# Splitting the tiled products of a linear-attention kernel into two runs

## The chip, the core and the metric

The kernel runs on one core of a Trainium2 chip. The metric is the time of one execution on the device in microseconds: 306.25 us, median of three runs (306.08 to 306.49). The core's engines that matter here are TensorE (PE, with its weight loads shown as PEld), VectorE (DVE), ScalarE (ACT), GpSimd (POOL) and SyncE (SP), which here only issues transfers. Each engine works through a queue of its own, and semaphores order the engines among each other.

## What is computed

The reference is a transformer stack of 12 layers of attention without softmax, followed by a layer norm, a gated FFN and another layer norm, on 16 sequences of 256 tokens with 128 features and 16 heads of 8 features. Cut to what matters:

```python
for i in range(12):
    q, k, v = split(x @ Wqkv[i].T + bqkv[i])          # 16 heads of 8
    att = einsum('bhqd,bhkd->bhqk', q, k) / sqrt(8)    # no softmax
    y = einsum('bhqk,bhkd->bhqd', att, v)
    x = y @ Wproj[i].T + bproj[i] + x
x = layernorm(x0 + x)
x = layernorm(x + (silu(x @ wg.T) * (x @ wu.T)) @ wd.T)
```

## The kernel before

Without a softmax a layer is linear in the tokens once `k` and `v` are summed over them. So the kernel never holds a layer's tokens. For every sequence it keeps a 128x128 matrix that maps the centred input tokens to the layer's tokens, and one more column for the offset (`tst`, 130 columns wide with padding; `thl` is its split into a high and a low part), and the Gram matrix of the input tokens (`g`). Two sequences form a pair (`PB = 2`), there are eight pairs (`NP`), and four pairs form a half (`G = 4`, `NO = 2` halves of eight sequences).

In each layer, and for each half, TensorE does the following work. "Full-size" are products that use all 128 rows and 128 columns of the array:

- **kv** (lines 436 to 438): six full-size products for each pair, which map `k` and `v` weights through the pair's matrices.
- **gv** (line 457): the Gram matrix times v's map, two fp32 products for each pair.
- **q** (lines 444 to 446): three full-size products for each pair, for q's map.
- **M** (line 501): k's map times the Gram product, that is keys against values, but only the diagonal blocks of 32x32 features. For a half these are 4 pairs x 2 sequences x 4 blocks = 32 matmuls, each on 128 rows and 32 columns of the array, so that four can lie side by side. They all write one bank, `pm`.
- **Offsets' products** (line 382, "riders"): eight small matmuls (twelve in layer 0), on 128x32 tiles too, that give the offsets of q, k and v for a half of this or of a later layer. They are issued in front of an M run.
- **y** (line 519): M, masked to heads (`gm`), times q's map. 2 sequences x 4 pairs x 4 blocks = 32 matmuls on 32x32 tiles of the array, sixteen of which can lie side by side. They write four banks, `pys`, one for each pair.
- **w** (lines 536 to 538): the output projection, three full-size products for each pair.

Between them VectorE, ScalarE and GpSimd move results out of the banks: `kv`, `gv` and `q` by copies (lines 205 and 207), M by an addition and a multiplication with the mask (lines 511 and 213) into `gm`, y by a split into `yhl` (lines 205 or 207, then 532), the projection by an addition to `tst` (line 543) with a split into `thl` (lines 205 and 210).

The order of all this isn't written by hand. Each step is an `Op` of a `Plan`, with its cost on each engine that may do it (in ns), what it reads and writes, and a priority. `Plan.run` goes through the steps like a simulator: it takes the step that can start first, by its own clock, breaks ties by priority, emits its instructions there and then, and so fixes the order on each engine, the engine where there's a choice, and the bank (eight of them). For a step on TensorE that follows another TensorE step it depends on, it takes a pause of 30 ns; after the other engines 300 ns. An M run with its riders is one step (cost 890 plus 140 for each rider), and so is a y run (cost 1200). A step's instructions are never mixed with those of another step on TensorE.

The riders of a half `o` in layer `l` are `(l, o)` for the first two layers, and `(l + o, 1 - o)` where that sum is from 2 to 11. So M has one rider in most runs, two in the second half of layer 1, and none in the second half of layer 11. What follows an M run's riders is in `offsets` (lines 385 to 405), ending with the addition on line 402 or 404.

When the eleven layers after layer 0 are done, `ffn` handles the eight pairs (line 575 on), which begins during layer 11.

Of the kernel before, what the change touches and what calls it, by code (L numbers as in the profile page):

```python
# [21 lines left out]
C = 128  # L22
# [3 lines left out]
PB = 2  # L26
NP = B // PB
W = C + 2
# [8 lines left out]
G = 4  # L37
# [13 lines left out]
LSTEP = 0.05  # L51
WLEAD = 0.6
TAILW = 0.0001
AHEAD = 0.16
SPARE = 500

# [17 lines left out]
PE, ACT, DVE, POOL, SP = "pe", "act", "dve", "pool", "sp"  # L74
AFTER = {PE: 270, ACT: 160, DVE: 200, POOL: 180, SP: 3000}
TO_PE = 300


class Val:


    def __init__(self, kind=None):
        self.kind, self.slot = kind, None
        self.writers, self.readers, self.ops, self.left = [], [], [], 0


class Op:
    def __init__(self, n, costs, emit, prio):
        self.n, self.costs, self.emit, self.prio = n, costs, emit, prio
        self.end = self.engine = None  # L90
        self.deps, self.users, self.vals = set(), [], []


class Plan:
    def __init__(self, slots):
        self.slots, self.ops = slots, []

    def op(self, costs, emit, reads=(), writes=(), prio=0.0):

        o = Op(len(self.ops), costs, emit, prio)  # L100
        for v in reads:
            o.deps.update(v.writers)
        for v in writes:
            o.deps.update(v.writers, v.readers)
            v.writers, v.readers = [o], []
        for v in reads:
            if v not in writes:
                v.readers.append(o)
        o.vals = list(dict.fromkeys([*reads, *writes]))
        for v in o.vals:  # L110
            if v.kind:
                v.left += 1
                v.ops.append(o)
        for d in o.deps:
            d.users.append(o)
        self.ops.append(o)

    def run(self):
        free = dict.fromkeys(AFTER, 0.0)
        free.update({SP: 800.0, DVE: 4000.0, ACT: 3200.0, POOL: 4900.0})  # L120
        slots = {k: [(0.0, i) for i in range(n)] for k, n in self.slots.items()}
        left = {o: len(o.deps) for o in self.ops}
        for o in reversed(self.ops):
            o.tail = min(o.costs.values()) + 300 + max((u.tail for u in o.users), default=0)
        ready = [o for o in self.ops if not left[o]]
        takes = lambda o: [v for v in o.vals if v.kind and v.slot is None]
        while ready:
            found = []
            for o in ready:
                if any(not slots[v.kind] for v in takes(o)):  # L130
                    continue
                held = max((min(slots[v.kind])[0] for v in takes(o)), default=0.0)
                best, least = None, None
                for e, c in o.costs.items():
                    t = max(free[e], held)
                    for d in o.deps:
                        wait = TO_PE if e == PE and d.engine in (ACT, DVE, POOL) else 30 if d.engine == e == PE else AFTER[d.engine]
                        t = max(t, d.end + wait)
                    rank = t + c + (SPARE if e == DVE and o.prio > L - 1.6 else 0)
                    if best is None or rank < least:  # L140
                        best, least = (t, t + c, e), rank
                found.append((best, o))
            assert found, "no slot is free"
            first = min(b[0] for b, _ in found)
            (_, end, e), o = min(((b, o) for b, o in found if b[0] <= first), key=lambda x: (x[1].prio - TAILW * x[1].tail, -x[1].tail, x[1].n))
            o.engine, o.end = e, end
            free[e] = end
            ready.remove(o)
            for v in takes(o):
                s = min(slots[v.kind])  # L150
                slots[v.kind].remove(s)
                v.slot = s[1]
            o.emit(e)
            for v in o.vals:
                if v.kind:
                    v.left -= 1
                    if not v.left:
                        slots[v.kind].append((max(x.end for x in v.ops) + 200, v.slot))
            for u in o.users:
                left[u] -= 1  # L160
                if not left[u]:
                    ready.append(u)
        assert all(o.end is not None for o in self.ops)
        self.span = max(free.values())
# [14 lines left out]
def dve(n, fast=False):  # L179
    return 69 + n / (1.92 if fast else 0.96)  # L180


def pool(n):
    return 147 + 2.1 * n
# [7 lines left out]
def linear_attention_ffn_kernel(ctx: ExitStack, tc: tile.TileContext, x, xt, wall, wq0, bias, wg, wu, wd, out):  # L192
    nc = tc.nc
    ctx.enter_context(tc.manual_schedule())
    sb = ctx.enter_context(tc.tile_pool(name="sb", bufs=1))
    ps = ctx.enter_context(tc.tile_pool(name="ps", bufs=1, space=PSUM))
    new = lambda name, shape, dt=F32: sb.tile([128, *shape], dt, name=name)

    plan = Plan({"bank": 8, "raw": RAW, "weights": WSLOTS, "turned": WSLOTS})
    banks = [ps.tile([128, 512], F32, name=f"bank{i}") for i in range(8)]  # L200
    bank = lambda v: banks[v.slot]
# [10 lines left out]
    def mul(e, dst, a, b):  # L212
        (nc.vector if e == DVE else nc.gpsimd).tensor_tensor(dst, a, b, ALU.mult)  # L213
# [55 lines left out]
    vq, vgv = [Val() for _ in range(NP)], [Val() for _ in range(NP)]  # L269
# [5 lines left out]
    wraw = [new(f"wraw{i}", [4 * C]) for i in range(RAW)]  # L275
# [43 lines left out]
    kvs = [new(f"kv{p}", [PB, 2, C]) for p in range(NP)]  # L319
    qss = [t[:, : PB * W].rearrange("p (a b) -> p a b", b=W) for t in qgvs]  # L320
    gvs = [t[:, PB * W :].rearrange("p (a b) -> p a b", b=C) for t in qgvs]
    yhl = [new(f"yhl{p}", [2, PB * W], F32R) for p in range(NP)]
    named = lambda: [Val() for _ in range(NP)]
    vt, vc, vhi, vlo, vm, vg0, vkv, vyh, vyl, vqo, vw = (named() for _ in range(11))
# [48 lines left out]
    def offset_products(l, o):  # L373

        raw, pc = wts[l][0], Val("bank")
        c = tst[:, o * OB : (o + 1) * OB, C]

        def mm():
            for s in range(1 if l else 0, 3):
                for g in range(G):  # L380
                    cols = slice(32 * g, 32 * g + 32)
                    nc.tensor.matmul(bank(pc)[cols, s * OB : (s + 1) * OB], wraw[raw.slot][:, s * C : (s + 1) * C][:, cols], c, start=True, stop=True)
        return [raw, *vc[o * G : (o + 1) * G]], pc, mm
# [34 lines left out]
    vgm = sets()  # L418
# [61 lines left out]
    def heads(l, o, prio, riders):  # L480

        raw = wts[l][0]
        pairs = range(o * G, (o + 1) * G)
        gm = gms[o]
        pm, pys = Val("bank"), [Val("bank") for _ in pairs]
        group = lambda g: slice(32 * (g % G), 32 * (g % G) + 32)
        src = [raw] if l == 0 else [vkv[p] for p in pairs]

        more = [(*r, *offset_products(*r)) for r in riders]

        def mm_m(e):
            for _, _, _, _, mm in more:
                mm()
            for p in pairs:
                for b in range(PB):
                    n = (p - o * G) * PB + b
                    tk = wraw[raw.slot][:, C : 2 * C] if l == 0 else kvs[p][:, b, 0, :]
                    for g in range(G):  # L500
                        nc.tensor.matmul(bank(pm)[group(g), n * 32 : n * 32 + 32], tk[:, group(g)], gvs[p][:, b, group(g)], start=True, stop=True)  # L501
        reads = [v for _, _, rs, _, _ in more for v in rs]
        if l == 0 and o == 1:

            reads += vw[:G]
        plan.op({PE: 890 + 140 * len(more)}, mm_m, [*(vgv[p] for p in pairs), *src, *reads], [pm, *(m[3] for m in more)], prio)
        for lo, oo, _, pc, _ in more:
            offsets(lo, oo, prio + (OFFSET if lo else 0), pc)
            if lo == 0:
                first_offsets(o, prio)  # L510
        plan.op({DVE: dve(OB * 32)}, lambda e: nc.vector.tensor_tensor(
            gm, bank(pm)[:, : OB * 32].rearrange("p (b j) -> p b j", j=32), kvo[:, o * OB : (o + 1) * OB], ALU.add), [pm, vkvo[o]], [vgm[o]], prio)
        plan.op({DVE: dve(OB * 32), POOL: pool(OB * 32)}, lambda e: mul(e, gm, gm, mask32.unsqueeze(1).to_broadcast([128, OB, 32])), [], [vgm[o]], prio)

        def mm_y(e):
            for b in range(PB):
                for r, p in enumerate(pairs):
                    for g in range(G):
                        nc.tensor.matmul(bank(pys[r])[group(g + r), b * W : (b + 1) * W], gm[group(g), r * PB + b, :], qss[p][group(g), b, :], start=True, stop=True)  # L519
        plan.op({PE: 1200}, mm_y, [vgm[o], *(vq[p] for p in pairs), *(vqo[p] for p in pairs)], pys, prio)  # L520
        return pys

    def projection(l, p, py, prio):
# [234 lines left out]
    for p in range(NP):  # L758
        ffn(p, L + FOFF + FSTEP * p - (AHEAD if p == NP - 1 else 0))
    plan.run()  # L760
# [31 lines left out]
```

## Time and profile before

| what | value |
|---|---|
| median of three runs | 306.25 us |
| the profiled execution | 306.32 us |
| its span, first to last instruction | 304.6 us |
| mean granted clock of TensorE | 0.996 |
| layers 1 to 11, about | 37 to 240 us |
| M's tile matmuls (line 501), records in those layers | 1408 |
| offsets' tile matmuls (line 382), records | 400 |
| y's tile matmuls (line 519), records | 1536 |

A matmul of fp32 operands leaves two records on PE and two on PEld. A record's start is when the instruction began; the length of a matmul's record includes its way through the array, so records that follow each other overlap: a full-size product has a length of 0.28 us, and the next one starts after 0.12 us. In a timeline, records of one line that follow each other are merged into one row with a count.

### The profile page before, as it was taken

Reading aid. Unit: us, or ns where it says so; the run is one execution under the profiler, and the core shown is the slowest. Engines: PE = TensorE matmul, PEld = TensorE weight load, DVE = VectorE, ACT = ScalarE, POOL = GpSimd, SP = SyncE. Lnnn points to the kernel's source line nnn. Section 1 sums busy time; section 2 is a strip of 40 time slices with the busy share of each in tenths; the row PEclk is TensorE's granted clock in tenths of the full one; section 3 lists DMA queues with packets and bytes.
Section 4 is the critical chain, followed back from the end, with each engine's and each line's share of the span. In section 5 each row is a group of like instructions: output and inputs, shape, how many; then the busy total and the mean of one; then the engine's idle time right before and its main releaser. Section 6 shows DMA issues by size and latency. Waiting matters only on the chain.

```text
span 304.6 us, 12894 instructions
## 1 busy us (share of the span) xinstructions
PE 295.0 (97%) x5382; PEld 270.8 (89%) x5382; DVE 226.6 (74%) x685; ACT 221.2 (73%) x564; POOL 140.7 (46%) x232
## 2 busy tenths in 40 slices
PE   8999999999999999999999999999999999989981
PEld 8989999999999999999999999999999898868870
DVE  4796877777677676876768777786545689999993
ACT  3556877767777768777686666876887567888875
POOL 6246352334531445215442254324433458767783
PEclk9999999999999999999999999999999999999998
DMA  7634213112031120311302102130000000000224
GB/s 209 156 101 126 71 39 88 38 46 81 3 88 37 40 89 3 88 40 31 95 2 56 37 21 61 33 80 4 2 2 3 4 1 2 0 0 2 70 69 139
DMA packets 22490, 15.66 MB, mean 51 GB/s; under 512 B 1952, under 2 KB 19872, under 8 KB 22432
## 3 DMA queue, kind: packets, MB, share of 16 engines
q1 hardware_dynamic: 21872, 14.62, 17.2%
q8 instruction: 42, 0.69, 1.0%
q10 hardware_dynamic: 560, 0.22, 0.3%
q14 instruction: 16, 0.13, 0.1%
HBM read 8.02 MB, written 2.10 MB: 33 GB/s over the span
## 4 chain that ended last, share of the span: by engine, by line
PE 81%; DVE 11%; ACT 3%; issue 3%; POOL 0%; POOLq 0%; DVEq 0%
PE bank L457 14%; PE bank L436 8%; PE bank L519 8%; PE bank L438 7%; PE bank L437 7%; PE bank L501 5%; PE bank L444 5%; PE bank L538 4%; PE bank L537 4%; PE bank L536 4%; PE bank L445 3%; PE bank L446 3%; PE bank L338 3%; DVE st L599 2%; DVE xt L704 2%
## 5 line engine op out<-in xcount | busy, mean ns | idle before, releaser
L210 POOL TENSOR_TENSOR thl<-tst,thl 128x260 fp32r<-128x260 f32 x88 | 64.9, 769 | 123.2 <-ACT thl L205 123.2
L205 ACT COPY qgv<-bank 128x256 f32<-128x256 f32 x170 | 60.8, 377 | 20.7 <-PE bank L446 13.4
L205 ACT COPY kv<-bank 128x512 f32<-128x512 f32 (+1 forms) x93 | 53.4, 577 | 18.8 <-PE bank L438 13.6
L436 PE MATMUL bank<-whl,thl 128*128 128x256 f32 x176 | 51.8, 294 | 0.0
L438 PE MATMUL bank<-whl,thl 128*128 128x256 f32 x176 | 49.7, 282 | 0.0
L437 PE MATMUL bank<-whl,thl 128*128 128x256 f32 x176 | 49.4, 281 | 0.0
L457 PE MATMUL bank<-kv,g 128*128 128x128 f32 x352 | 46.0, 275 | 0.0
L543 DVE TENSOR_TENSOR tst<-bank,tst 128x260 f32<-128x260 f32 x96 | 36.9, 425 | 11.2 <-PE bank L538 9.0
L205 ACT CAST thl<-tst 128x260 fp32r<-128x260 f32 x88 | 33.1, 410 | 14.5 <-DVE tst L543 14.4
L457 PEld LDWEIGHTS bank<-kv,g 128*128 128x128 f32 x352 | 42.7, 191 | 0.4 <-issue 0.4
L450 DVE TENSOR_SCALAR qgv<-bank,bcol 128x2 f32<-128x2 f32 x88 | 19.3, 221 | 27.8 <-ACT qgv L205 23.4
L532 DVE TENSOR_TENSOR yhl<-bank,yhl 128x260 fp32r<-128x260 f32 x96 | 34.5, 421 | 3.0 <-ACT yhl L205 3.0
L436 PEld LDWEIGHTS bank<-whl,thl 128*128 128x128 f32 x176 | 33.1, 188 | 4.1 <-issue 3.8
L438 PEld LDWEIGHTS bank<-whl,thl 128*128 128x128 f32 x176 | 33.1, 188 | 0.2 <-POOL thl L210 0.2
L437 PEld LDWEIGHTS bank<-whl,thl 128*128 128x128 f32 x176 | 33.2, 189 | 0.0
L444 PE MATMUL bank<-thl,whl 128*128 128x260 f32 x88 | 28.9, 328 | 0.0
L519 PE MATMUL bank<-qgv,gm 32*32 32x130 f32 x1536 | 25.8, 280 | 0.2 <-DVE gm L213 0.2
L205 ACT CAST yhl<-bank 128x260 fp32r<-128x260 f32 (+1 forms) x62 | 22.4, 412 | 4.7 <-PE bank L519 4.5
L207 DVE CAST yhl<-bank 128x260 fp32r<-128x260 f32 x42 | 16.1, 424 | 12.9 <-PE bank L519 12.9
L445 PE MATMUL bank<-thl,whl 128*128 128x260 f32 x88 | 24.8, 282 | 0.0
L446 PE MATMUL bank<-thl,whl 128*128 128x260 f32 x88 | 24.7, 281 | 0.0
L519 PEld LDWEIGHTS bank<-qgv,gm 32*32 32x32 f32 x1536 | 17.2, 103 | 5.5 <-ACT kv L205 0.3
(155 smaller groups left out, 704.3 us busy)
## 6 DMA issues: line engine op xcount, KB each, us to landing
wraw<-wall SPq DMA_DIRECT2D x12, 256.0 KB, 2.9
wpt<-whl SPq DMA_DIRECT2D x24, 96.0 KB, 2.2
qgv<-x SPq DMA_DIRECT2D x8, 256.0 KB, 5.2
xt<-xt SPq DMA_DIRECT2D x8, 256.0 KB, 3.2
out<-kv SPq DMA_DIRECT2D x7, 256.0 KB, 2.3
wpt<-whl SPq DMA_DIRECT2D x24, 64.0 KB, 2.6
wpt<-whl SPq DMA_DIRECT2D x24, 32.0 KB, 1.9
wraw<-wg SPq DMA_DIRECT2D x1, 192.0 KB, 3.6
```

Of the source, the lines that this page charges most:

```text
L205: nc.scalar.copy(dst, src)
L210: (nc.vector if e == DVE else nc.gpsimd).tensor_tensor(dst, a, b, ALU.subtract)
L436: nc.tensor.matmul(o, hi[:, b, 0:C], hl(0, 1, 2), start=True, stop=False)
L437: nc.tensor.matmul(o, hi[:, b, 0:C], hl(1, 1, 2), start=False, stop=False)
L438: nc.tensor.matmul(o, lo[:, b, 0:C], hl(0, 1, 2), start=False, stop=True)
L444: nc.tensor.matmul(o, hl(0, 0), flat(hi), start=True, stop=False)
L445: nc.tensor.matmul(o, hl(0, 0), flat(lo), start=False, stop=False)
L446: nc.tensor.matmul(o, hl(1, 0), flat(hi), start=False, stop=True)
L457: nc.tensor.matmul(bank(pgv)[:, b * C : (b + 1) * C], g0[p][:, b, :], tv(b), start=True, stop=True)
L519: nc.tensor.matmul(bank(pys[r])[group(g + r), b * W : (b + 1) * W], gm[group(g), r * PB + b, :], qss[p][group(g), b, :], start=True, stop= ...
L532: plan.op({DVE: dve(PB * W)}, lambda e: nc.vector.tensor_tensor(yl, bank(py)[:, : PB * W], yh.bitcast(F32), ALU.subtract), [py, vyh[p]], [ ...
L543: plan.op({DVE: dve(PB * W)}, lambda e: nc.vector.tensor_tensor(ts, bank(pw)[:, : PB * W], ts, ALU.add), [pw], [vt[p], vc[p]], prio)
```

## The change

M's step and y's step are each divided into two steps of half the matmuls. M's first step does the half's first two pairs, its second step the other two pairs; the riders' products go with the second. y's first step does the first sequence of each of the four pairs, its second step the second sequence. M stays whole in layer 0, and y in the first half of layer 0. The planner gets a new parameter for a step, `apart`: the pause in its clock between two TensorE steps that depend on each other, 300 for the second step of M and of y, so that it puts other steps that are ready in between; 30 otherwise. The costs that the planner takes for the steps are new as well: 430 for half an M, 100 for each rider, 520 for half a y.

```diff
+APART = 300
 class Op:
-    def __init__(self, n, costs, emit, prio):
+    def __init__(self, n, costs, emit, prio, apart):
...
-    wait = TO_PE if e == PE and d.engine in (ACT, DVE, POOL) else 30 if d.engine == e == PE else AFTER[d.engine]
+    wait = TO_PE if e == PE and d.engine in (ACT, DVE, POOL) else o.apart if d.engine == e == PE else AFTER[d.engine]
...
-        src = [raw] if l == 0 else [vkv[p] for p in pairs]
-        def mm_m(e):
-            for _, _, _, _, mm in more:
-                mm()
-            for p in pairs:
...
-        plan.op({PE: 890 + 140 * len(more)}, mm_m, [*(vgv[p] for p in pairs), *src, *reads], [pm, *(m[3] for m in more)], prio)
+        runs = [pairs] if l == 0 else [pairs[: G // 2], pairs[G // 2 :]]
+        for ps in runs:
+            last = ps is runs[-1]
+            def mm_m(e, ps=ps, last=last):
+                for _, _, _, _, mm in more if last else []:
+                    mm()
+                for p in ps:
...
+            reads = [v for _, _, rs, _, _ in more for v in rs] if last else []
+            src = [raw] if l == 0 else [vkv[p] for p in ps]
+            cost = (890 if l == 0 else 430) + (140 if l == 0 else 100) * len(more) * last
+            plan.op({PE: cost}, mm_m, [*(vgv[p] for p in ps), *src, *reads], [pm, *(m[3] for m in more if last)], prio, APART if last and l else 30)
...
-        def mm_y(e):
-            for b in range(PB):
-                for r, p in enumerate(pairs):
...
-        plan.op({PE: 1200}, mm_y, [vgm[o], *(vq[p] for p in pairs), *(vqo[p] for p in pairs)], pys, prio)
+        for run in ([range(1), range(1, PB)] if l + o else [range(PB)]):
+            def mm_y(e, run=run):
+                for b in run:
+                    for r, p in enumerate(pairs):
...
+            plan.op({PE: 520 if l + o else 1200}, mm_y, [vgm[o], *(vq[p] for p in pairs), *(vqo[p] for p in pairs)], pys, prio, APART if run[0] else 30)
```

In the order that results, a half of a middle layer reads on TensorE, with the number of products (for tile runs: of matmuls): before, `q 9, riders 8 + M 32, q 3, kv 12, y 32, kv 12, gv 2, w 12, gv 6`; after, `M 16, q 6, riders 8 + M 16, q 6, kv 12, y 16, kv 6, y 16, kv 6, gv 4, w 12, gv 4`.

More of the change, by code (lines that the diff above doesn't have):

```diff
@@ L87 @@
 class Op:
-    def __init__(self, n, costs, emit, prio):
-        self.n, self.costs, self.emit, self.prio = n, costs, emit, prio
+    def __init__(self, n, costs, emit, prio, apart):
+        self.n, self.costs, self.emit, self.prio, self.apart = n, costs, emit, prio, apart
         self.end = self.engine = None
@@ L96, in __init__, with op @@
         self.slots, self.ops = slots, []
-    def op(self, costs, emit, reads=(), writes=(), prio=0.0):
-        o = Op(len(self.ops), costs, emit, prio)
+    def op(self, costs, emit, reads=(), writes=(), prio=0.0, apart=30):
+        o = Op(len(self.ops), costs, emit, prio, apart)
         for v in reads:
@@ L488, in heads @@
         group = lambda g: slice(32 * (g % G), 32 * (g % G) + 32)
-        src = [raw] if l == 0 else [vkv[p] for p in pairs]
         more = [(*r, *offset_products(*r)) for r in riders]
-        def mm_m(e):
-            for _, _, _, _, mm in more:
-                mm()
-            for p in pairs:
-                for b in range(PB):
[L498 to L505, printed above, removed]
-        plan.op({PE: 890 + 140 * len(more)}, mm_m, [*(vgv[p] for p in pairs), *src, *reads], [pm, *(m[3] for m in more)], prio)
+        runs = [pairs] if l == 0 else [pairs[: G // 2], pairs[G // 2 :]]
[5 more added lines that the diff above has]
+                for p in ps:
+                    for b in range(PB):
+                        n = (p - o * G) * PB + b
+                        tk = wraw[raw.slot][:, C : 2 * C] if l == 0 else kvs[p][:, b, 0, :]
+                        for g in range(G):
+                            nc.tensor.matmul(bank(pm)[group(g), n * 32 : n * 32 + 32], tk[:, group(g)], gvs[p][:, b, group(g)], start=True, stop=True)
+            reads = [v for _, _, rs, _, _ in more for v in rs] if last else []
+            if l == 0 and o == 1:
+                reads += vw[:G]
+            src = [raw] if l == 0 else [vkv[p] for p in ps]
+            cost = (890 if l == 0 else 430) + (140 if l == 0 else 100) * len(more) * last
+            plan.op({PE: cost}, mm_m, [*(vgv[p] for p in ps), *src, *reads], [pm, *(m[3] for m in more if last)], prio, APART if last and l else 30)
         for lo, oo, _, pc, _ in more:
@@ L513, in heads @@
         plan.op({DVE: dve(OB * 32), POOL: pool(OB * 32)}, lambda e: mul(e, gm, gm, mask32.unsqueeze(1).to_broadcast([128, OB, 32])), [], [vgm[o]], prio)
-        def mm_y(e):
-            for b in range(PB):
-                for r, p in enumerate(pairs):
-                    for g in range(G):
-                        nc.tensor.matmul(bank(pys[r])[group(g + r), b * W : (b + 1) * W], gm[group(g), r * PB + b, :], qss[p][group(g), b, :], start=True, stop=True)
-        plan.op({PE: 1200}, mm_y, [vgm[o], *(vq[p] for p in pairs), *(vqo[p] for p in pairs)], pys, prio)
+        for run in ([range(1), range(1, PB)] if l + o else [range(PB)]):
+            def mm_y(e, run=run):
+                for b in run:
+                    for r, p in enumerate(pairs):
+                        for g in range(G):
+                            nc.tensor.matmul(bank(pys[r])[group(g + r), b * W : (b + 1) * W], gm[group(g), r * PB + b, :], qss[p][group(g), b, :], start=True, stop=True)
+            plan.op({PE: 520 if l + o else 1200}, mm_y, [vgm[o], *(vq[p] for p in pairs), *(vqo[p] for p in pairs)], pys, prio, APART if run[0] else 30)
         return pys
```

## The prediction

> **What bounds the kernel now.** I read the busy shares first, then the windows, then TensorE's waits, and last the timeline of TensorE around one y run and one M run. Busy shares (engine, us, share of the span, instructions), then three windows (from:to, length, busy time and instructions of PE, PEld, DVE, ACT, POOL, then clock, DMA share, GB/s):
>
> ```profile
> PE 295.0 (97%) x5382; PEld 270.8 (89%) x5382; DVE 226.6 (74%) x685; ACT 221.2 (73%) x564; POOL 140.7 (46%) x232
> ...
> 0.00:37.00 37.00, 35.74 (x688) 33.46 (x689) 25.32 (x105) 21.77 (x56) 18.29 (x56) 1.00 0.49 136
> 37.00:240.00 203.00, 202.83 (x4304) 190.41 (x4303) 145.64 (x449) 149.05 (x392) 77.87 (x117) 1.00 0.15 42
> 240.00:304.60 64.60, 56.41 (x394) 46.94 (x392) 55.64 (x133) 50.34 (x119) 44.59 (x60) 0.98 0.12 34
> ```
>
> From 37 to 240 us, where nearly all of layers 1 to 11 lie, TensorE stands still for 0.17 us of 203. Its list of waits for others holds six rows, and only the last two lie in the layers; the others are the start and the FFN:
>
> ```profile
> PE bank L538 <- DVE yhl L532: 0.2, 1, 0.2
> PE bank L519 <- DVE gm L213: 0.2, 1, 0.2
> ```
>
> So a microsecond added to TensorE's stream there is a microsecond of the kernel. What the stream pays for tile runs stands in the timeline (start, length, engine, line, operation, shapes, how many records; an fp32 matmul leaves two). First a whole y run, then the same run cut after its first 32 records, then its other 32:
>
> ```profile
> 102.95 0.28 PE L437 MATMUL bank<-whl,thl 128*128 128x256 f32 x1
> 103.07 0.28 PE L438 MATMUL bank<-whl,thl 128*128 128x256 f32 x1
> 103.28 1.07 PE L519 MATMUL bank<-qgv,gm 32*32 32x130 f32 x64
> 104.28 0.38 PE L436 MATMUL bank<-whl,thl 128*128 128x256 f32 x1
> 104.50 0.28 PE L437 MATMUL bank<-whl,thl 128*128 128x256 f32 x1
> 104.62 0.29 PE L438 MATMUL bank<-whl,thl 128*128 128x256 f32 x1
> ...
> 103.28 0.50 PE L519 MATMUL bank<-qgv,gm 32*32 32x130 f32 x32
> ...
> 103.60 0.75 PE L519 MATMUL bank<-qgv,gm 32*32 32x130 f32 x32
> ```
>
> Then an M run with one set of offsets' products, and one without, whole and cut after 32 records:
>
> ```profile
> 100.26 0.28 PE L446 MATMUL bank<-thl,whl 128*128 128x260 f32 x1
> 100.47 0.31 PE L382 MATMUL bank<-tst,wraw 128*32 128x8 f32 x16
> 100.62 0.75 PE L501 MATMUL bank<-qgv,kv 128*32 128x32 f32 x64
> 101.30 0.39 PE L444 MATMUL bank<-thl,whl 128*128 128x260 f32 x1
> 101.53 0.28 PE L445 MATMUL bank<-thl,whl 128*128 128x260 f32 x1
> ...
> 236.65 0.76 PE L501 MATMUL bank<-qgv,kv 128*32 128x32 f32 x64
> ...
> 236.65 0.46 PE L501 MATMUL bank<-qgv,kv 128*32 128x32 f32 x32
> ```
>
> The reader sees two things. Full-size products start every 0.12 us (102.95, 103.07; 104.50, 104.62), but on both sides of a tile run that step is longer: 0.21 into it (103.07 to 103.28), and behind it the first full product starts late and its successor 0.22 later (104.28 to 104.50), since its weight load starts with it and not one step ahead. And within a y run the first 16 matmuls are issued at once, the other 16 come slowly.
>
> **The price of a run, part by part** (starts from the records, to the ns). A y run, from the last full product before it to the second behind it, takes 1.436 us; two ordinary steps (0.239) would pass there anyway, so the run costs 1.197. From its first to its last tile matmul pass 0.805 (1.07 less the last one's own 0.269), so 0.392 is the price of going in and out. The halves: the first 32 records span 0.50 - 0.269 = 0.235; the other 32 span 0.75 - 0.269 = 0.485, after a gap of 0.085. In the slow half one matmul comes every 16.7 ns. A queue ahead of TensorE that holds some 16 fp32 matmuls and is filled no faster than that would give this picture.
>
> An M run with one rider: 100.26 to 101.53 is 1.268, less 0.239 is 1.029; its tile matmuls span 0.706; going in and out costs 0.323 (less than y's, as the last matmul streams 32 columns and not 130). Without a rider the span is 0.76 - 0.196 = 0.566, and its first half 0.46 - 0.196 = 0.262. So M's first half is hardly faster than its second (0.304 with the gap): M's four column tiles take about 16 ns for a matmul with a full queue too. The first 48 records of a rider's run (8 offsets' products and 16 of M's) span 0.406.
>
> **What the change does to it.** Before, TensorE's order holds 48 tile runs (24 of M, 24 of y), each between full-size products. After, it holds 93: M's 22 of layers 1 to 11 and 23 of y's fall in two, with 6 full products in between in most layers (y: one pair's L436 to L438; M: two pairs' L444 to L446), in the others 2 to 24. No instruction is added or removed; no two halves end up side by side.
>
> - y, 23 times: before 1.197; after, if both halves issue like the first, 2 x (0.235 + 0.392) = 1.254. The faster half saves 0.335, the second going in and out takes 0.392: +0.057 each, +1.3 in all.
> - M with one rider, 20 times: before 1.029; after 0.262 + 0.323 and 0.406 + 0.323, together 1.314: +0.285. With two riders once (48 matmuls span 0.865 in layer 1, its first 32 span 0.565): 0.585 + 0.888 against 1.188, also +0.285; without, once: 2 x 0.585 against 0.889, +0.28. Together +6.3.
>
> What does the price of going in and out consist of, and can the new runs pay less? From the y run: 0.09 more than a step on the way in; 0.11 of streaming by the last matmul and 0.09 after it before the full weight load starts; 0.10 of that load, in the open. The way in is passed with the queue full (a long stretch of full products stands ahead of it) and has the same 0.09 as the way out, where the queue is empty: so this part doesn't come from the queue. That the load isn't made earlier could come from the queue, since every run of before ends starved: no row shows a way out with a full queue. One bound is therefore 0.104 less for each of 90 runs, -9.4 us; the other is nothing less. I take nothing less: after a slow y run the load's turn comes 17 ns behind the last tile matmul, and it still waits for 0.18 more, to 0.09 past the end of that matmul's streaming.
>
> [...]
>
> Refilling: between halves lie 0.36 us or more of full products; at 16.7 ns that is 21 matmuls, more than the 16 needed. If not, y's second half would take 0.485 again, 0.25 more.
>
> Moved work. M to y: six q and twelve kv products stand between (before: three and twelve), so `gm`'s two operations gain cover. y to the projection: six kv and four gv products, 1.6 us, where 1.9 stood; the last low part of y ends at 106.39 and is first read at 107.58, so of 1.2 us of slack 0.9 stays. M's second run reads gv copies covered by M's first run and six q products, 1.3 us against nine q products, 1.1. Without that cover each would stall TensorE by the missing tenths, 22 times. Eight of the 0.31 us adds of the offsets (L402, ScalarE) go to GpSimd (L404), with the low parts of tokens (L210) queued behind, that L438 waits for; GpSimd is idle 123 us in front of these, so nothing; without that cover 8 x 0.31 = 2.5. SyncE's queue changes by one transfer. In the FFN a few copies, each 0.5 to 0.7 us, change between VectorE, ScalarE and GpSimd in both directions: ±1 us, taken as nothing.
>
> **Sum.** +6.3 + 1.3 = +7.6 us against the profiled execution, 306.32 us (span 304.6 and 1.7 around it; the median of the runs is 306.25): 313.9.
>
> **Rivals.**
> - Faster, one mechanism: behind a short run the queue isn't empty, and the full weight load is made in the drain's shadow. 90 x 0.104 less than the sum: 304.5. For it: no row shows such a way out. Against it: the waiting load at 104.28. It decides from 0.084 less for each run (7.6 / 90).
> - Faster still: the planner's new costs in the diff hold (y 520 twice for 1200, M 430 and 530 for 1030). They would give 23 x -0.16, 20 x -0.07, -0.11 and -0.03: -5.2, or 301.1. For it: its old costs are just what the timeline gives (1.197, 1.029). Against: 430 leaves 0.17 for M's way in and out, where 0.323 stands.
> - Something between, with a part of the load hidden: 306 to 311.
> - Slower still: the queue isn't refilled; 23 x 0.25 more, 319.7. Against it: the refill time above.
>
> **How the numbers follow.** The forecast 0.66 (its own range 311.5 to 316, from the FFN's ±1 and stalls of a few tenths in some layers); the hidden load 0.15; between 0.08, half of it within 0.2% (0.6 us, about what a measurement of this kernel tells from no change); the planner's costs 0.06; no refill 0.05. Faster 0.21, same 0.04, slower 0.75. From 304.0 to 316.5 the range takes in the forecast, what lies between and most of the hidden load, and leaves out under 0.2.
>
> **What the profile after would show.** Right: y's runs as x32 with a length near 0.50 and M's near 0.46, each entered 0.21 after a full product; the first full product behind each followed by the next after 0.22; TensorE without idle time to about 247 us. The forecast is wrong if that 0.22 is 0.12 (the hidden load), if y's second run is 0.75 long (no refill), or if TensorE waits between 37 and 240.

## The result, and the profile after

The changed kernel takes 314.57 us (median of four runs, 314.25 to 314.97), the kernel before 306.37 on the same chip: a ratio of 1.0268, with a 95% interval from 1.0251 to 1.0284, or 8.2 us more. The profiled executions are 314.25 and 306.32 us, with spans of 312.5 and 304.6.

The diff moves the line numbers: y is now line 528, M 506, the riders 384, kv 438 to 440, q 446 to 448, gv 459, the mask's multiplication 215. The busy shares of the changed kernel:

```profile
PE 302.7 (97%) x5382; PEld 269.0 (86%) x5382; DVE 225.9 (72%) x685; ACT 220.2 (70%) x567; POOL 141.7 (45%) x238
```

Its window from 37 to 240 us (columns as before):

```profile
37.00:240.00 203.00, 202.32 (x4204) 181.56 (x4203) 139.87 (x435) 142.21 (x373) 77.51 (x109) 1.00 0.16 42
```

The whole kernel leaves the same 5382 matmul records, and TensorE is as busy as before: it waits little for others (0.7 us of these 203, where it was 0.2), it needs longer. In 203 us it gets 100 records less done. In the timeline of TensorE the two halves of a y run and the two halves of an M run look like this (a full-size product of kv or q leaves one record, a tile matmul two):

```profile
115.77 0.28 PE L440 MATMUL bank<-whl,thl 128*128 128x256 f32 x1
115.98 0.50 PE L528 MATMUL bank<-qgv,gm 32*32 32x130 f32 x32
116.42 0.39 PE L438 MATMUL bank<-whl,thl 128*128 128x256 f32 x1
116.64 0.28 PE L439 MATMUL bank<-whl,thl 128*128 128x256 f32 x1
...
117.32 0.50 PE L528 MATMUL bank<-qgv,gm 32*32 32x130 f32 x32
...
111.78 0.46 PE L506 MATMUL bank<-qgv,kv 128*32 128x32 f32 x32
112.17 0.39 PE L446 MATMUL bank<-thl,whl 128*128 128x260 f32 x1
112.40 0.28 PE L447 MATMUL bank<-thl,whl 128*128 128x260 f32 x1
...
113.09 0.31 PE L384 MATMUL bank<-tst,wraw 128*32 128x8 f32 x16
113.24 0.46 PE L506 MATMUL bank<-qgv,kv 128*32 128x32 f32 x32
```

Both halves of y are now 0.50 long, the slow 0.75 is gone. But each is entered 0.21 behind a full product (115.77 to 115.98), and the second full product behind it comes 0.22 after the first (116.42 to 116.64), as behind the long runs of before. M's halves are 0.46 long, as the first half was within the whole run.

| term | predicted | measured |
|---|---|---|
| M with one rider | +0.285 each | 0.819 + 0.974, less four steps of 0.1195, against 1.029: +0.286 |
| M, 22 runs | +6.3 | +6.3 |
| y, 23 runs | +0.057 each, +1.3 | 0.866 + 0.865, less four steps, against 1.197: +0.056, +1.3 |
| stalls in front of y | nothing | 0.39, 0.39 and 0.11, less one of 0.24 before: +0.65 |
| from the last y run to the end | nothing, ±1 | 61.2 us before, 60.9 after: -0.3 |
| sum | +7.6 | +7.9 (314.25 against 306.32) |

The terms are medians over all runs of a kind, from the last full product before a run to the second behind it. One of the three stalls, with what TensorE waited for in brackets (0.60 from product to run in place of 0.21):

```profile
105.27 0.28 PE L440 MATMUL bank<-whl,thl 128*128 128x256 f32 x1
105.87 0.52 PE L528 MATMUL bank<-qgv,gm 32*32 32x130 f32 x32 [0.32 <-DVE qgv L452]
```

L452 is VectorE's addition of an offset to q; why it comes late is shown under "The planner's costs" below.

### The profile page after: what moved, and what is told of

It reads as the page before. It is cut to its first block, busy times and chain, and to the rows that moved or that the text cites. A ratio compares the mean times of both kernels' runs of the same rounds, so it can differ in the third digit from the quotient of the medians.

```text
span 312.5 us, 13011 instructions
## 1 busy us (share of the span) xinstructions
PE 302.7 (97%) x5382; PEld 269.0 (86%) x5382; DVE 225.9 (72%) x685; ACT 220.2 (70%) x567; POOL 141.7 (45%) x238
## 4 chain that ended last, share of the span: by engine, by line
PE 88%; DVE 7%; ACT 2%; issue 1%; POOLq 0%; ACTq 0%; POOL 0%
PE bank L459 14%; PE bank L438 9%; PE bank L528 7%; PE bank L440 6%; PE bank L439 6%; PE bank L446 6%; PE bank L506 5%; PE bank L547 4%; PE bank L546 4%; PE bank L545 4%; PE bank L447 3%; PE bank L448 3%; PE bank L340 2%; PE bank L709 2%; PE bank L710 2%; PE bank L384 2%
## 5 line engine op out<-in xcount | busy, mean ns | idle before, releaser
L207 ACT COPY qgv<-bank 128x256 f32<-128x256 f32 x174 | 64.2, 377 | 33.1 <-PE bank L448 24.2
L207 ACT COPY kv<-bank 128x512 f32<-128x512 f32 (+1 forms) x91 | 52.2, 576 | 27.4 <-PE bank L440 20.8
L438 PE MATMUL bank<-whl,thl 128*128 128x256 f32 x176 | 53.6, 305 | 0.0
L440 PE MATMUL bank<-whl,thl 128*128 128x256 f32 x176 | 49.6, 282 | 0.0
L439 PE MATMUL bank<-whl,thl 128*128 128x256 f32 x176 | 49.5, 281 | 0.0
L459 PE MATMUL bank<-kv,g 128*128 128x128 f32 x352 | 47.1, 277 | 0.0
L452 DVE TENSOR_SCALAR qgv<-bank,bcol 128x2 f32<-128x2 f32 x88 | 19.3, 219 | 30.6 <-ACT qgv L207 27.1
L552 DVE TENSOR_TENSOR tst<-bank,tst 128x260 f32<-128x260 f32 x96 | 35.9, 424 | 5.3 <-PE bank L550 2.3
L207 ACT CAST thl<-tst 128x260 fp32r<-128x260 f32 x88 | 32.3, 409 | 10.2 <-DVE tst L552 10.1
L209 DVE CAST yhl<-bank 128x260 fp32r<-128x260 f32 (+1 forms) x42 | 16.4, 430 | 25.1 <-PE bank L528 25.0
L446 PE MATMUL bank<-thl,whl 128*128 128x260 f32 x88 | 29.4, 334 | 0.0
L528 PE MATMUL bank<-qgv,gm 32*32 32x130 f32 x1536 | 24.4, 281 | 0.7 <-DVE qgv L452 0.6
L447 PE MATMUL bank<-thl,whl 128*128 128x260 f32 x88 | 25.0, 284 | 0.0
L448 PE MATMUL bank<-thl,whl 128*128 128x260 f32 x88 | 24.8, 282 | 0.0
L624 POOL TENSOR_TENSOR rs<-ve,mhalf 128x4 f32<-128x4 f32 x16 | 16.9, 1056 | 8.1 <-DVE ve L611 5.4
```

What stands on the lines that cost most here:

```text
L207: nc.scalar.copy(dst, src)
L438: nc.tensor.matmul(o, hi[:, b, 0:C], hl(0, 1, 2), start=True, stop=False)
L439: nc.tensor.matmul(o, hi[:, b, 0:C], hl(1, 1, 2), start=False, stop=False)
L440: nc.tensor.matmul(o, lo[:, b, 0:C], hl(0, 1, 2), start=False, stop=True)
L446: nc.tensor.matmul(o, hl(0, 0), flat(hi), start=True, stop=False)
L447: nc.tensor.matmul(o, hl(0, 0), flat(lo), start=False, stop=False)
```

## The experiments

Each kernel is compared with the kernel before on the same chip. The edits under "Each part alone", "The queue behind a run" and "The planner's costs" are made to the changed kernel, the others to the kernel before.

### Each part alone

In the first kernel only y's loop of the change is kept, in the second only M's; the planner has the old costs for what stays whole.

```diff
-        runs = [pairs] if l == 0 else [pairs[: G // 2], pairs[G // 2 :]]
+        runs = [pairs]
...
-        for run in ([range(1), range(1, PB)] if l + o else [range(PB)]):
+        for run in [range(PB)]:
```

The first edit gives the one kernel, the second the other, each with its cost.

> Only y in two runs, M whole with its old cost. Theory (each extra run pays the way in and out, 0.392 us, and gets 0.335 back from the faster half): +0.057 for 23 runs, +1.3 us against the kernel before, 0.4% slower. Rival (the loss of the whole change comes from its order and stalls and is shared by both parts): about half of +8.2, +4. Rival (the planner's costs hold): -3.7.

> Only M in two runs, y whole with its old cost. Theory: +0.285 for 22 runs, +6.3 us against the kernel before, as M's halves issue no faster than the whole. Rival (shared by both parts): about +4. Rival (the planner's costs hold): -1.5. If the parts add up, this and the y-only kernel together lose what the whole change loses, 8.2, less its two or three stalls of 0.4 us.

Measured: y alone 308.06 against 306.56, ratio 1.0051 (1.0032 to 1.0070), +1.5 us; M alone 312.31 against 306.56, ratio 1.0183 (1.0167 to 1.0200), +5.8. The theory had +1.3 and +6.3; the interval of M's loss, 5.1 to 6.1 us, ends a little below 6.3. The parts add up to 7.3, and the whole change lost 8.2, with the three stalls that neither part has to that extent. So the loss isn't shared: it follows the runs of each kind, and the planner's new costs do not describe either part.

### The queue behind a run

y in four runs of eight matmuls, for each of which the planner takes 570; M whole, with its old cost.

```diff
-        for run in ([range(1), range(1, PB)] if l + o else [range(PB)]):
+        for i, (run, rs) in enumerate([(range(b, b + 1), rs) for b in range(PB) for rs in ((0, 1), (2, 3))] if l + o else [(range(PB), range(G))]):
```

> y in four runs of 8 matmuls, M whole. With 8 matmuls of some 16 in the queue, the full product behind a run is surely queued when the run ends. Theory (the way in and out is the drain and an open weight load, whatever the queue holds): 4 x (0.18 + 0.392) = 2.29 us for a y against 1.197, +1.09 for 23, +25 us against the kernel before. Rival (a load that is queued is hidden): 0.104 less for each of 92 runs, +15.5.

Measured: 334.07 against 306.56, ratio 1.0893 (1.0870 to 1.0917), +27.5 us. This is the first rival of the prediction, the weight load hidden behind a short run, put to the test. In the timeline of this kernel:

```profile
104.45 0.28 PE L440 MATMUL bank<-whl,thl 128*128 128x256 f32 x1
104.66 0.45 PE L528 MATMUL bank<-qgv,gm 32*32 32x130 f32 x16
105.04 0.39 PE L438 MATMUL bank<-whl,thl 128*128 128x256 f32 x1
105.26 0.28 PE L439 MATMUL bank<-whl,thl 128*128 128x256 f32 x1
```

The steps 0.21 and 0.22 are still there around a run of only 16 records, and so are the 0.20 us from the last tile matmul's start (104.84, as its own record is 0.27 of the 0.45) to the full product, the drain of the theory. The price of going in and out is the same for a run of 8 matmuls, which by the prediction's estimate of some 16 leaves room in the queue for the product behind it; the rival's +15.5 falls. (Of the 2.5 us above the +25 of the theory 1.6 are waits in front of M: its runs with a rider take 1.35 on the mean and 1.27 in the kernel before.)

### How long the queue takes to fill

The order of the kernel before, with one full-size product between y's halves, which computes nothing.

```diff
             for b in range(PB):
+                if b and l + o:
+                    nc.tensor.matmul(bank(pys[0])[:, 260:512], zero, apart, start=True, stop=True)
```

> The kernel before, its order unchanged, but between the two halves of a y run from layer 0's second half on stands one full-size bf16 product of 252 columns with zeros, into unused columns of y's bank: it adds a product that computes nothing. Theory (a mode change and some 0.5 us are enough to fill the queue again): both halves span 0.235, the run with its product costs about 1.35 against 1.197, +3 to +4 us for 23 runs. Rival (it takes several full products, 0.3 us and more, to fill the queue): the second half stays at 0.485, +9 us.

Measured: 307.83 against 306.30, ratio 1.0048 (1.0029 to 1.0067), +1.5 us.

```profile
104.38 0.28 PE L440 MATMUL bank<-whl,thl 128*128 128x256 f32 x1
104.58 0.50 PE L523 MATMUL bank<-qgv,gm 32*32 32x130 f32 x32
105.02 0.28 PE L520 MATMUL bank<-apart,zero 128*128 128x252 bf16 x1
105.23 0.50 PE L523 MATMUL bank<-qgv,gm 32*32 32x130 f32 x32
105.67 0.38 PE L438 MATMUL bank<-whl,thl 128*128 128x256 f32 x1
105.89 0.28 PE L439 MATMUL bank<-whl,thl 128*128 128x256 f32 x1
```

Both halves are 0.50 long: one product and two mode changes (0.20 us from the last tile matmul's start to the product on the full array, and 0.21 back to tiles) are enough for a second half as fast as the first, in the theory's reading to fill the queue, and the six products that the change put between halves are not needed for that. The theory's size was too high. It charged the extra product's weight load in the open, 0.1 us; the row shows the step from that product to the next tile run at 0.21 as elsewhere, so a run costs 1.51 - 0.24 = 1.27 and not 1.35.

### What a split can give back

y's operands are bf16 from layer 1 on, in the order of the kernel before: one pass for each matmul, so half the records. The two writes of q into `qsb`, a bf16 view of q's tile, are not shown here.

```diff
-        plan.op({...}, lambda e: mul(e, gm, gm, mask32...), [], [vgm[o]], prio)
+        plan.op({...}, lambda e: mul(e, gmb[o] if l else gm, gm, mask32...), [], [vgm[o]], prio)
...
-    nc.tensor.matmul(bank(pys[r])[...], gm[group(g), r * PB + b, :], qss[p][group(g), b, :], start=True, stop=True)
+    nc.tensor.matmul(bank(pys[r])[...], (gmb[o] if l else gm)[group(g), r * PB + b, :], (qsb[p] if l else qss[p])[group(g), b, :], start=True, stop=True)
```

> The kernel before, its order unchanged, but from layer 1 on y's operands are bf16, so that a matmul is one pass (two records in all) and not two (four records). It leaves out precision: y is computed from operands rounded to bf16. Theory (the queue holds 64 records, 16 fp32 matmuls): all 32 matmuls of a run fit and start 7 ns apart, the span of a run falls from 0.805 to about 0.21, the price in and out to about 0.34 as the last matmul streams half as long; a y run costs 0.55 and not 1.197, -15 us for 23 runs. Rival (the queue holds 16 matmuls, whatever their passes): the second 16 come every 16.7 ns, span 0.37, -11 us. Rival (the second half is slow because it uses the same tiles again): the slow half stays at half its length, span near 0.4 with 0.04 gaps, -9 us or less.

Measured: 289.77 against 306.30, ratio 0.9468 (0.9442 to 0.9494), -16.5 us.

```profile
97.58 0.28 PE L440 MATMUL bank<-whl,thl 128*128 128x256 f32 x1
97.79 0.34 PE L526 MATMUL bank<-qgv,gmb 32*32 32x130 bf16 x32
98.05 0.39 PE L438 MATMUL bank<-whl,thl 128*128 128x256 f32 x1
98.27 0.28 PE L439 MATMUL bank<-whl,thl 128*128 128x256 f32 x1
```

A whole run of 32 matmuls spans 0.12 us, one start every 4 ns (123 ns over 31 steps) and no slow half, though every tile is used twice. From the full product before a run to the second behind it 0.70 pass, where 1.44 passed: 0.74 less for 22 runs is 16.2, nearly all of the gain. Going in and out takes 0.34 of the 0.70 (less two steps, 0.24, and the span), as the theory had it. (The theory, with starts 7 ns apart, had a span of 0.21 and a gain of 15 us for 23 runs; there are 22.) So what starved y's second half was the number of records ahead of it, not the second use of the tiles; in fp32 too the 32 records of the fast half use each of the 16 tiles twice, once in each pass. In fp32 the fast part ended after 16 matmuls; with half the records for each, all 32 pass. This kernel beats both, at the price of y's precision; one pass on operands with more bits wasn't tried. The queue itself shows in no trace. The theory's 64 records are the author's estimate from the run of before: 16 fp32 matmuls in its fast half, each with two records on PE and two on PEld. The 32 one-pass matmuls, with one record on PE and one on PEld each, leave as many, and their run has no slow part.

Then the same kernel with a product of zeros between the halves:

> y's operands in bf16 from layer 1 on, as in the one-pass kernel (it leaves out the same precision), and y's run in two halves with one full-size product of zeros between them. Theory (what a split gives back is only the starved half, and one pass leaves none): the halves' spans add up to the whole's 0.12, and the full price in and out, about 0.34 with the product, is lost for 23 runs: +7.5 to +8 us against the one-pass kernel, 297 to 298. Rival (a split gives something back beside the queue, as early tiles or banks): +2 us, as between the kernel with the gap and the kernel before.

Measured: 297.51 against 306.06, ratio 0.9725 (0.9703 to 0.9746). Against the one-pass kernel's 0.9468 that is 2.6% of the time before, 7.9 us, lost again, within the theory's 7.5 to 8.

```profile
100.45 0.28 PE L442 MATMUL bank<-whl,thl 128*128 128x256 f32 x1
100.66 0.28 PE L530 MATMUL bank<-qgv,gmb 32*32 32x130 bf16 x16
100.87 0.28 PE L527 MATMUL bank<-apart,zero 128*128 128x252 bf16 x1
101.08 0.28 PE L530 MATMUL bank<-qgv,gmb 32*32 32x130 bf16 x16
101.29 0.38 PE L440 MATMUL bank<-whl,thl 128*128 128x256 f32 x1
101.51 0.28 PE L441 MATMUL bank<-whl,thl 128*128 128x256 f32 x1
```

1.06 us pass here from the full product to the second behind the run (100.45 to 101.51), 0.36 more than for the undivided run, and the tile rows hardly pay for it: each half spans 0.05 us, where the whole took 0.12. Where there's no starved half, a split loses nearly the whole way in and out. Beside the queue it gives next to nothing back.

### The planner's costs, and a held multiplication

The whole change, with the durations that the runs have in the planner.

```diff
-            cost = (890 if l == 0 else 430) + (140 if l == 0 else 100) * len(more) * last
+            cost = (890 if l == 0 else 585) + 140 * len(more) * last
...
-            plan.op({PE: 520 if l + o else 1200}, mm_y, ...)
+            plan.op({PE: 627 if l + o else 1200}, mm_y, ...)
```

> The whole change, but the planner takes the durations that the runs have: 627 for half a y, 585 for half an M, 140 for a rider. Theory (the price is in the 45 extra runs, the order hardly matters): the two stalls of 0.39 us in front of y go, 0 to 1 us below the changed kernel, still 7 to 8 us above the kernel before. Rival (the too low costs made the order that loses): most of the 8 us come back.

Measured: 317.98 against 306.56, ratio 1.0363 (1.0345 to 1.0381), 11.4 us slower than before and some 3 slower than the change. That fits neither expectation: the true costs made a worse order. In the window from 37 to 240 us TensorE stands still for 0.5 us only, but in six of the eleven layers one half of a y run looks like the first row here. The second row is GpSimd's, the third and fourth VectorE's, each from its own timeline of this kernel; the last is from the list of what weight loads waited for (us in total, times, longest):

```profile
107.66 0.92 PE L528 MATMUL bank<-qgv,gm 32*32 32x130 f32 x32
...
105.94 1.30 POOL L212 TENSOR_TENSOR whl<-wraw,whl 128x512 fp32r<-128x512 f32 x1
...
106.24 1.28 DVE L215 TENSOR_TENSOR gm<-gm,mask 128x256 f32<-128x256 f32 x1
107.44 0.21 DVE L452 TENSOR_SCALAR qgv<-bank,bcol 128x2 f32<-128x2 f32 x1
...
PEld bank L528 <- DVE qgv L452: 1.7, 6, 0.3
```

The half is 0.92 long and not 0.50: it starts, and stops in the middle for 0.28 us. GpSimd takes 1.30 us to subtract the low part of a layer's weights, from 105.94 to 107.24. VectorE's multiplication of `gm` with the mask starts 0.30 later, takes 1.28 where its median is 0.42, and ends 0.28 after GpSimd's. Behind it on VectorE stand the offsets of q (L452), which y's last matmuls read. From 85 to 189 us the multiplication takes 1.28 six times, once in each layer, and each time a half of y is 0.42 longer: 2.5 us. (The span, 316.2, is 3.7 above the changed kernel's. y's halves account for 2.2 of that; 1.2 lies ahead of them, before layer 0's second y run, and wasn't followed up.) In the changed kernel the two meet too: from 60 us on, four times the multiplication takes 0.92 or 0.93, which is hidden, once 1.04, with the stall of 0.11, and twice 1.32, with the two of 0.39. That VectorE is held by GpSimd's instruction was tried by cutting that one up in the kernel with the true costs, with the order unchanged:

```diff
-        plan.op({POOL: pool(n)}, lambda e: sub(e, whl[hl.slot][:, 1, a:], ...), [raw, *after], [hl], prio)
+        def low(e):
+            for i in range(a, 4 * C, C):
+                sub(e, whl[hl.slot][:, 1, i : i + C], ...)
+        plan.op({POOL: pool(n)}, low, [raw, *after], [hl], prio)
```

> The kernel with the planner's true costs, its order unchanged, but GpSimd subtracts a layer's weights' low part in four instructions of 128 columns and not in one of 512. Theory (in that kernel the mask's multiplication on VectorE, line 215, is held for as long as one GpSimd instruction that started before it, 1.28 us and not 0.42, and y then waits 0.42 within a run in most layers): with short instructions it is held 0.4 at most, the stalls go, -2.5 to -3.5 us against the kernel with the true costs (near 315). Rival (the stall has another cause, or GpSimd as such slows VectorE, however long its instructions are): no change, 318.

Measured: 314.54 against 306.06, ratio 1.0278 (1.0260 to 1.0296), so 0.85% or 2.6 us better than with one long instruction. GpSimd's and VectorE's rows of the same moment in this kernel's timelines:

```profile
104.66 1.90 POOL L212 TENSOR_TENSOR whl<-wraw,whl 128x128 fp32r<-128x128 f32 x4
...
104.94 0.46 DVE L215 TENSOR_TENSOR gm<-gm,mask 128x256 f32<-128x256 f32 x1
```

And all of these multiplications, from the view by tile (ns: least, median, most; then first and last start in us):

```profile
L215 DVE TENSOR_TENSOR gm<-gm,mask x20: 412/424/674, 24.8 to 215.9; 128x256 f32<-128x256 f32 x20
```

The four pieces take 1.90 us instead of 1.30, and still the multiplication never takes more than 0.67. From full product to second full product y's halves take 0.868 on the mean, no more than their median, where the mean was 0.931 with the long instruction. So it is the length of the one GpSimd instruction that VectorE is held for, not GpSimd being at work. With these stalls away the true costs give about the time of the change (ratios 1.0278 and 1.0268), which still holds 0.9 us of them: the order from the true costs brings none of the 8 us back.

## Why the prediction was right

It forecast 313.9 us and a range of 304.0 to 316.5; 314.57 was measured.

- **The bound.** TensorE's stream sets the time from 37 us on, and what is added there is added to the kernel. Right: a layer lasts 19.5 us before and 20.2 after, and the sum of the runs' prices is the loss.
- **The price of going in and out**, read off the long runs and taken over for the short ones, held to a few ns (0.21 in, 0.22 after), with 8, 16, 24 and 32 matmuls in a run. The step that a row couldn't show, a way out with a full queue, was decided for the end that costs, and the four-run kernel shows that this was the right end. One part of the price, 0.11 us of streaming by the last matmul, stood there without a row, as the author's estimate. The lengths of the tile matmuls' records before (0.176 us with 8 columns, 0.196 with 32, 0.269 with 130) give about 0.10 for 130 columns, an estimate too (0.073 for the last 98 of them). The one-pass kernel agrees: its last record is 0.22 long (0.34 less 0.12), and from its start to the next full product pass 0.14 us in place of 0.20, less by about half of the 0.11.
- **y's gain.** The second half did become as fast as the first (0.235 us, the median of 46 halves), and the 0.335 that this gives back don't pay for 0.392.
- **M's lack of a gain.** Right: M's tile matmuls issue hardly faster at the start of a run (0.262 us for the first half, 0.304 for the second with the gap before it), and the halves by themselves are 0.46 long, like the first half of the whole run, so M's split loses nearly its whole price, five sixths of the total.
- **The planner's new costs** were rejected because 430 leaves too little for M's way in and out. The measured halves cost 0.58 and 0.74, y's 0.63.
- **What was missed.** Moved work was costed at nothing with the cover named, and one such cover had a hole: `gm`'s operations gained three products of cover on TensorE, but the multiplication met a long GpSimd instruction on which it was held, up to 1.32 us, where the longest case before was 0.80. That put 0.65 us on top. By the letter one of the prediction's own signs of being wrong came true with it, since TensorE waited 0.7 us between 37 and 240; the prediction had allowed for stalls of a few tenths in its own range, but put nothing in the sum and didn't name this cause.
- The FFN's end was taken as nothing with ±1, and gave 0.3 back. So part of how close the number came is luck: the sum is out by +0.65 and -0.3, neither of them foreseen, and the profiled execution the sum speaks of took 314.25.

## What to carry to other kernels

Before a run of small tile matmuls is cut, two numbers are to be read in its timeline: how much longer the steps before and behind the run are than an ordinary step, and by how much the run's tail is slower than its head. Only where the second exceeds the first does a cut pay; here it was 0.335 against 0.392 for y and 0.04 against 0.32 for M. The better cure for a starved tail is fewer records for each matmul: one pass in place of two took 0.74 us off each run, at the price of y's precision, where the cut added 0.06. And an order that a planner makes has collisions that its costs don't know, so a change of costs is to be judged by the stalls that appear, not by how true the costs are.

## What the runs showed of the hardware that wasn't expected

In the kernel with the true costs, VectorE's multiplication of `gm` with the mask takes 1.28 us in place of 0.42 when it starts 0.30 us after a GpSimd instruction of 1.30 us, and with GpSimd's work in pieces at most 0.67. The long one ends 0.28 us after GpSimd's instruction. That is less than its own 0.42, so it wasn't held for all of that time. What in that instruction holds it, no run shows. The wait reaches TensorE not through the multiplication, but through the small instruction queued behind it on VectorE (L452, at 107.44), for which a half of y stops in the middle for 0.28 us.
